# A recommender model on one core: the end of the GRU loop with its last softmax blocks in PSUM, an item term by TensorE and the last poolings divided differently

## The chip, the cores and the metric

The kernel runs on one core of one Trainium2 chip. The metric is the device time of one execution in microseconds, less being better. A core has TensorE (PE in the profile, its weight loads PEld), VectorE (DVE), ScalarE (ACT), GpSimd (POOL) and SyncE (SP), each with its own queue of instructions, which it works off in order; they meet through semaphores. Operands lie in SBUF, 128 partitions wide, or in PSUM, eight banks into which TensorE writes. In this kernel GpSimd works on SBUF alone.

## What is computed

1024 users have a history of 100 items, each a vector of 128. A GRU runs over the history, an attention gives each step a score against a target item, a masked softmax over the steps weights the GRU's states, and the pooled result sets the update gate of a second recurrence (AUGRU) over the same states. A small network makes the final score. Cut to what matters here:

```python
_, gru_seq = jax.lax.scan(gru_step, h0, jnp.swapaxes(item_historical_embedding, 0, 1))
keys = jnp.swapaxes(gru_seq, 0, 1)
q = jnp.broadcast_to(item_embedding[:, None, :], keys.shape)
feat = jnp.concatenate([keys, q, keys - q, q * keys], axis=-1)
score = _mlp(feat, [(att_W0, att_b0), (att_W1, att_b1), (att_W2, att_b2)], jax.nn.relu)
score = jnp.where(mask[:, :, None] == 1, score, -jnp.inf)
attn = jax.nn.softmax(score, axis=1)[..., 0]
pooled = jnp.einsum('bt,btd->bd', attn, keys)
att_seq = pooled.T[:T]
...
_, aug_seq = jax.lax.scan(augru_step, h0, (jnp.swapaxes(keys, 0, 1), att_seq))
```

The first attention layer has a part that depends on the step (keys, and keys times item) and a part that depends on the item alone.

## The kernel before, in words

Features lie on the partitions and users along the free axis, in two halves of 512 users. The kernel has two phases. `gru_phase` runs 100 GRU steps over both halves (`Half.gru`), and beside them the attention, the softmax, the pooling, and what the final network can have early. `augru_phase` runs the second recurrence, which needs the pooled weights of all users: it starts with a store of `pooled` to memory, gathers of its rows, and their spreading by TensorE. The schedule is written by hand: the order of the calls in the source is the order in each engine's queue.

The attention of a step takes three rounds. `attend(t)` lets TensorE make, in 32-column blocks that share one bank per half, the first layer of step t (`wk` with the state, `wkq` with the product state times item), the second layer of step t-1 and the third of step t-2, all in one pass over the `mv` of the round before. `take(t)` reads the result: up to step 99 VectorE adds the item part `q0`, which was made once for all steps with its bias (L684, `f`), ScalarE applies the Relu (L689, `mv`), and the finished score of step t-2 goes by DMA on SP from a row of `mv` into `s_b` (L696). The rounds T and T+1 finish the last two steps; there ScalarE reads the bank itself, with a bias (L691).

The softmax goes by blocks of steps whose ends are in `ENDS`: the last are 90 to 93, 93 to 96, 96 to 98 and 98 to 100. A block has three stages: scores of half 0, scores of half 1 with the maxima, and, after an exponential on ScalarE, the sums. As the maximum can rise, a block also gives a factor by which what has been pooled so far is scaled. `Half.pool` then works off a list per half: a scaling (L576) when a block begins, and for each step a product of the transposed state with the weight (L586) and an addition to `pooled` (L587), the two called a pair below. Each half has its own part of `pooled`, in which the additions follow one another. Within the loop GpSimd pools.

After the loop six PSUM banks are taken over, `b[0]` to `b[5]`. The blocks 96 to 98 and 98 to 100 then have their weights `e` in PSUM (`banks["e"]`; named `last` in the profile) and are copied to SBUF at the end of their sums (L773), so that VectorE pools from PSUM and GpSimd from SBUF. The block 93 to 96 is begun inside the loop and has its `e` in SBUF; a copy of it to PSUM is made for VectorE (L885). Half 0 is then pooled by GpSimd and half 1 by VectorE (L890 to L914). Between these, TensorE makes the features of the final network (L617, `some`), and the last transposes of the state are made (L537). At the end VectorE masks `pooled` into `s_b` (L919), and SP and ScalarE send the result to memory.

Whether VectorE or GpSimd works off an entry, and where, is said by calls such as these:

```python
halves[0].pool(T, nc.gpsimd)
halves[1].pool(1, nc.vector)
stage()
```

The count is the number of steps to pool at most; scalings on the way are not counted.

Of the kernel before, what the change touches and what calls it, by code (L numbers as in the profile page):

```python
# [9 lines left out]
F32 = mybir.dt.float32  # L10
# [9 lines left out]
P = 128  # L20
B = 1024
T = 100
HB = 512
# [6 lines left out]
NK = B // R  # L30
# [7 lines left out]
QA, QB = (2, 3), (3, 2)  # L38
# [10 lines left out]
ENDS = (*range(8, 81, 8), 86, 90, 93, 96, 98, T)  # L49


G = 4
# [20 lines left out]
def kernel(ctx: ExitStack, tc: tile.TileContext, a: dict, out: bass.AP):  # L73
# [26 lines left out]
    nc = tc.nc  # L100
# [22 lines left out]
    item = const.tile([P, B], F32, name="item")  # L123
# [47 lines left out]
    def gru_phase(pools):  # L171
# [18 lines left out]
        wk, wkq, wq, w12, bm = [], [], [], [], []  # L190
# [447 lines left out]

        banks = {}

        def attend(t):

            p = left[t] = [pa.tile([P, HB], F32, tag="a", name="pm") for _ in halves]

            old = [half.mv if t else hist[:, half.cols] for half in halves]
            k_rows = slice(0 if t <= T else 2 * R, P)

            def pack(i, q, w, v, start, stop):
                s = ts(q, R)
                nc.tensor.matmul(p[i][s, :], lhsT=w[:, s], rhs=v, start=start, stop=stop)  # L650

            def first(i, q, j):
                if t < T:
                    w = (wk, wkq)[j][i]
                    pack(i, q, w, halves[i].first[j], j == 0 and q != QB[i], j == 1)

            def more(i, q):
                pack(i, q, w12[i][k_rows, :], old[i][k_rows, :], True, q == QA[i] or t >= T)

            for turn in range(2 * NH):  # L660
                i, j = divmod(turn, 2)
                for q in range(2):
                    first(i, q, j)
                if i == 0:
                    for q in range(2, P // R):
                        more((QA, QB)[j].index(q), q)
                else:
                    for q in range(2, P // R):
                        first(QB.index(q), q, j)
# [1 line left out]
        blocks = [0, *ENDS]  # L671
        soft = {"stages": [], "exp": None, "j": 0}

        def take(t):

            if t < 0:
                return
            p = left.pop(t)
            rows = slice(0 if t < T else 2 * R, P)
            sums = []  # L680
            for half in halves:
                if t < T:
                    sums.append(wp.tile([P, HB], F32, name="f"))
                    nc.vector.tensor_add(sums[-1], p[half.i], q0[:, half.cols])  # L684
            for half in halves:
                half.mv = wp.tile([P, HB], F32, name="mv", bufs=4)
                to, of, bias = half.mv[rows, :], p[half.i][rows, :], bm[half.i][rows, :]
                if t < T:
                    nc.scalar.activation(to, sums[half.i], AF.Relu)  # L689
                else:  # L690
                    nc.scalar.activation(to, of, AF.Relu, bias=bias)  # L691
            s, j = t - 2, soft["j"]
            if s < 0:
                return
            for half in halves:
                nc.sync.dma_start(  # L696
                    out=s_bs[NH * (j % 2) + half.i].rearrange("(p r) f -> p r f", r=R)[
                        :, s - blocks[j], :
                    ],
                    in_=half.mv[SC[half.i] : SC[half.i] + 1, :]  # L700
                    .unsqueeze(1)
                    .to_broadcast([1, P // R, HB]),
                )
            if s == blocks[j + 1] - 1:
                softmax()


        def softmax():

            j = soft["j"]  # L710
            b0, b1 = blocks[j], blocks[j + 1]
            n, last = b1 - b0, b1 == T
            rows = n + (1 if j else 0)
            on = later["on"][:, :, b0:b1]
            top_old, den_old = soft.get("top"), soft.get("den")
            e = sp.tile([P, NK, 2 * G + 1], F32, name="e", bufs=3)
            both = e, None
            if banks:

                b = banks["e"].pop()  # L720
                both = e, b[:, : NK * (G + 1)].rearrange("p (k n) -> p k n", n=G + 1)
                e = both[1]
                top_n, den_n = (b[:, NK * m : NK * (m + 1)] for m in range(G + 1, G + 3))
            top = sp.tile([P, NK], F32, name="top", bufs=3)
            den = sp.tile([P, NK], F32, name="den", bufs=3)
            if both[1] is None:
                top_n, den_n = top, den
            soft.update(j=j + 1, top=top, den=den, e=both)

            def scores(i):  # L730
                ks = ts(i, KH)
                if banks:
                    pt = blocked(banks["pt"])
                else:
                    pt = pa.tile([P, KH, R], F32, tag="a", name="pt")
                nc.vector.transpose(
                    pt, s_bs[NH * (j % 2) + i].rearrange("p (k r) -> p k r", r=R)
                )

                nc.vector.tensor_mul(e[:, ks, :n], pt[:, :, :n], on[:, ks, :])  # L740

            def tops():
                scores(1)
                nc.vector.tensor_reduce(top_n, e[:, :, :n], AX.X, ALU.max)
                if j:
                    nc.vector.tensor_max(top, top_n, top_old)
                    nc.vector.tensor_sub(e[:, :, n], top_old, top_n)
                    if both[1] is not None:
                        nc.vector.tensor_scalar_min(e[:, :, n], e[:, :, n], 0.0)
                nc.vector.tensor_sub(  # L750
                    e[:, :, :n], e[:, :, :n], top.unsqueeze(2).to_broadcast([P, NK, n])
                )
                soft["exp"] = exponents

            def exponents():
                nc.scalar.activation(e[:, :, :rows], e[:, :, :rows], AF.Exp)

            def sums():
                nc.vector.tensor_mul(e[:, :, :n], e[:, :, :n], on)  # L759
                nc.vector.tensor_reduce(den_n, e[:, :, :n], AX.X, ALU.add)  # L760
                if j:
                    old = sp.tile([P, NK], F32, name="old")
                    nc.vector.tensor_mul(old, den_old, e[:, :, n])
                    nc.vector.tensor_add(den, den_n, old)
                if last:
                    nc.vector.reciprocal(den, den)
                    nc.vector.tensor_mul(
                        e[:, :, :rows],
                        e[:, :, :rows],
                        den.unsqueeze(2).to_broadcast([P, NK, rows]),  # L770
                    )
                if both[1] is not None:
                    nc.vector.tensor_copy(both[0][:, :, :rows], e[:, :, :rows])  # L773
                for half in halves:
                    if j:
                        half.todo.append((both, n, None))
                    half.todo += [(both, t - b0, t) for t in range(b0, b1)]

            soft["stages"] += [lambda: scores(0), tops, sums]

        def stage(count=1):
            for _ in range(count):
                if soft["stages"]:
                    soft["stages"].pop(0)()
# [72 lines left out]
        all_of(rest)  # L857

        b = [ps.tile([P, HB], F32, tag="g", name="last") for _ in range(6)]
        banks.update(e=[b[0], b[1]], kw=b[3], pt=b[2], f=[b[4], b[5]])  # L860

        features = [half.features(g) for half in halves for g in range(GH)]

        def some(*these):
            for f in these:
                next(features[f])

        take(T - 2)
        for half in halves:
            half.product(T - 1)  # L870
        attend(T - 1)
        stage(2)
        weights = soft["e"][0]
        exponents()
        some(0, 1)
        take(T - 1)
        some(0, 1)
        attend(T)
        some(2)
        for half in halves:  # L880
            half.transpose(T - 1)
        stage()
        n = ENDS[-3] - ENDS[-4] + 1
        copy = banks["e"][0][:, : NK * n].rearrange("p (k n) -> p k n", n=n)
        nc.vector.tensor_copy(copy, weights[:, :, :n])  # L885
        for half in halves:
            half.todo = [
                ((w[0], copy if w[0] is weights else None), n, t) for w, n, t in half.todo
            ]
        halves[0].pool(T, nc.gpsimd)  # L890
        halves[1].pool(1, nc.vector)
        stage()
        take(T)
        some(2)
        attend(T + 1)
        some(3, 4)
        stage()
        take(T + 1)
        exponents()
        some(3, 4)  # L900
# [8 lines left out]
        stage(2)  # L909
        exponents()  # L910
        some(7)
        stage()
        halves[0].pool(T, nc.gpsimd)
        halves[1].pool(T, nc.vector)  # L914


        for half in reversed(halves):
# [372 lines left out]
```

## Time and profile before

| what | us |
|---|---|
| median of 5 runs | 2089.94 |
| lowest and highest of them | 2086.67, 2091.57 |
| the profiled execution | 2088.85 |
| its span in the profile | 2087.1 |
| last GRU state written (L527) | 1413.08 |
| VectorE's last work of the first phase (L919) begins | 1446.70 |
| VectorE's first work of the second phase (L973) | 1461.40 |

A line of the timeline has the start in us from the span's beginning, the duration in us, the engine, the line of the kernel, the operation, output and inputs with their shapes, and a count. Brackets give how long the engine was idle before and what released it. Equal neighbours are merged, so that an x2 stands for two instructions. An instruction can begin while the end of the one before it is still counted, so what lies from one start to the next is used for chains of them. In a row of a stretch, the busy time of each engine is followed by its count of instructions.

### The profile page before, as it was taken

How to read it: one execution, taken by the hardware profiler on the slowest of the kernel's cores; microseconds unless marked ns; L12 is line 12 of the kernel's file. 1: busy time of each engine (PE TensorE's matmuls, PEld its weight loads, DVE VectorE, ACT ScalarE, POOL GpSimd, SP SyncE). 2: the span in 40 equal slices, each digit the busy share in tenths (PEclk: the TensorE clock that was granted, in tenths of full speed). 3: DMA queues.
4: the chain of work that ended last, by engine and by line, in shares of the span. 5: the costliest groups of instructions: out<-in, count | busy, mean ns of one | idle time of the engine just before them, and what ended most of it. 6: DMA issues, size and time to landing. Idle time of an engine off the chain costs nothing. (4 is left out here: it accounts for less than half of the span.)

```text
span 2087.1 us, 26811 instructions
## 1 busy us (share of the span) xinstructions
PE 2040.4 (98%) x8320; PEld 981.4 (47%) x8320; DVE 1753.7 (84%) x3050; ACT 832.3 (40%) x1516; POOL 1308.9 (63%) x1306
## 2 busy tenths in 40 slices
PE   8999999999999999999999999997899999999997
PEld 3343333333333333333333333333444556679887
DVE  6888999999989888989888899997467777888786
ACT  3334343433434333433343343343344444455454
POOL 0334939579796959595969687986635444444232
PEclk9999999999999999999999999999999999999999
DMA  4643233332234334333433232332534333334231
GB/s 118 114 93 99 91 103 110 95 103 84 87 103 111 114 98 121 110 100 104 133 108 91 82 92 79 101 93 74 148 95 111 97 93 96 98 98 100 74 73 35
DMA packets 254324, 205.09 MB, mean 98 GB/s; under 512 B 75814, under 2 KB 216842, under 8 KB 254170
## 3 DMA queue, kind: packets, MB, share of 16 engines
q1 hardware_dynamic: 239738, 170.57, 29.4%
q0 software_dynamic: 12320, 32.44, 5.6%
q8 instruction: 68, 1.11, 0.2%
q14 instruction: 86, 0.70, 0.1%
q10 hardware_dynamic: 2112, 0.26, 0.1%
HBM read 147.16 MB, written 54.40 MB: 97 GB/s over the span
## 5 line engine op out<-in xcount | busy, mean ns | idle before, releaser
L490 PE MATMUL ps<-x,wih 128*128 128x512 f32 x1200 | 592.6, 603 | 4.2 <-DMA x<-in_hist_x 4.2
L490 PE MATMUL ps<-hn,whh 128*128 128x512 f32 x1188 | 574.4, 592 | 0.0
L490 PEld LDWEIGHTS ps<-x,wih 128*128 128x128 f32 x1200 | 220.9, 191 | 327.7 <-issue 253.2
L490 PEld LDWEIGHTS ps<-hn,whh 128*128 128x128 f32 x1188 | 225.7, 190 | 284.1 <-issue 275.3
L476 POOL TENSOR_TENSOR xm<-x,m 128x512 f32<-128x512 f32 x200 | 248.6, 1243 | 135.2 <-DMA m<-mask_d 134.9
L521 ACT ACTIVATE ps<-ps,bih 128x512 f32<-128x512 f32 x200 | 132.4, 662 | 480.2 <-DVE ps L520 480.2
L502 ACT ACTIVATE r<-ps,brz 128x512 f32<-128x512 f32 x200 | 137.5, 687 | 380.8 <-PE ps L490 380.2
L477 POOL TENSOR_TENSOR hist<-hist,xm 128x512 f32<-128x512 f32 x200 | 269.0, 1345 | 15.7
L586 POOL TENSOR_TENSOR kw<-kt,e 128x512 f32<-128x512 f32 x191 | 219.5, 1149 | 70.3 <-DVE e L759 70.2
L587 POOL TENSOR_TENSOR pooled<-pooled,kw 128x512 f32<-128x512 f32 x191 | 254.0, 1330 | 15.0
L159 POOL DMA_INDIRECT rows<-keys_d,idx_k x208 | 202.8, 975 | 83.8 <-POOL rows L158 51.5
L563 DVE TENSOR_TENSOR kq<-hn,item 128x512 f32<-128x512 f32 x200 | 226.5, 1171 | 0.0
L650 PE MATMUL pm<-hn,wk 128*32 128x512 f32 x1200 | 211.6, 596 | 3.5 <-ACT q L233 1.8
L650 PE MATMUL pm<-kq,wkq 128*32 128x512 f32 x1200 | 209.2, 592 | 0.0
L1032 ACT ACTIVATE c<-ph,bh 128x96 f32<-128x96 f32 (+42 forms) x198 | 96.9, 489 | 263.3 <-PE ph L1024 229.7
L650 PE MATMUL pm<-mv,w 128*32 128x512 f32 (+1 forms) x808 | 195.8, 598 | 0.6 <-DVE e L740 0.6
L158 POOL COPY rows<-rest 128x1 f32<-128x1 f32 x208 | 39.4, 190 | 224.1 <-DVE rest L1061 219.9
L1048 DVE TENSOR_TENSOR pu<-pu,c 128x96 f32<-128x96 f32 (+42 forms) x197 | 88.8, 451 | 105.1 <-ACT c L1032 89.5
L684 DVE TENSOR_TENSOR f<-pm,q 128x512 f32<-128x512 f32 x200 | 128.3, 683 | 51.8 <-PE pm L650 51.8
L525 DVE TENSOR_TENSOR d<-hn,ps 128x512 f32<-128x512 f32 x198 | 136.0, 687 | 34.8 <-ACT ps L521 32.5
L526 DVE TENSOR_TENSOR d<-ps,d 128x512 f32<-128x512 f32 x200 | 138.3, 691 | 23.7 <-ACT ps L522 6.8
L520 DVE TENSOR_TENSOR ps<-ps,u 128x512 f32<-128x512 f32 x200 | 140.0, 700 | 21.6 <-PE ps L490 0.5
(180 smaller groups left out, 3031.4 us busy)
## 6 DMA issues: line engine op xcount, KB each, us to landing
x<-in_hist_x SPq DMA_DIRECT2D x212, 256.0 KB
keys_d<-kt SPq DMA_DIRECT2D x46, 1024.0 KB
m<-mask_d SPq DMA_DIRECT2D x200, 128.0 KB
keys_d<-kt SPq DMA_DIRECT2D x64, 64.0 KB
rows<-keys_d,idx_k POOLq DMA_INDIRECT x208
s_b<-mv SPq DMA_DIRECT2D x200, 8.0 KB
mask_i<-in_mask SPq DMA_DIRECT2D x8, 200.0 KB
at<-att_d SPq DMA_DIRECT2D x32, 48.0 KB
```

What stands on the lines that cost most here:

```text
L159: nc.gpsimd.indirect_dma_start(out=r[:, k, :], out_offset=None, in_=keys_d[q], in_offset=bass.IndirectOffsetOnAxis(ap=idx_k[:, k, i : i + ...
L476: nc.gpsimd.tensor_mul(d, x, m)
L477: nc.gpsimd.tensor_add(acc, acc, d)
L490: nc.tensor.matmul(p, lhsT=w[:, g, :], rhs=v, start=(j == 0), stop=(j == len(parts) - 1),)
L502: nc.scalar.activation(r, pr, AF.Sigmoid, bias=brz[:, 0:1])
L520: nc.vector.tensor_add(pi, pi, u)
L525: nc.vector.tensor_sub(d, h, pi)
L526: nc.vector.tensor_mul(d, pz, d)
L563: nc.vector.tensor_mul(kq, h, item[:, self.cols])
L586: eng.tensor_mul(d, k, w)
L587: eng.tensor_add(acc, acc, d)
L650: nc.tensor.matmul(p[i][s, :], lhsT=w[:, s], rhs=v, start=start, stop=stop)
```

## The change

- The block 93 to 96 no longer begins inside the loop (the test behind L704 leaves its end out); `softmax()` is called for it after the loop, when the banks are there. So its scores, maxima, weights and sums lie in PSUM, and the copy at the end of its sums goes to SBUF. L885 and what belongs to it goes.
- Three blocks need three places for `e`: one bank is divided in two for the blocks 93 to 96 and 96 to 98. The last block uses `b[0]`.
- The attention of the last step, `attend(T - 1)`, gets banks of its own (`b[0]` and `b[3]`) instead of the two used in turn. TensorE adds the item part to them first, six 32-column matmuls of `wq` with `item`; `take(T - 1, own=True)` therefore has no addition by VectorE, and ScalarE reads the banks with the bias.
- This `take` now stands ahead of the exponential of the block 93 to 96 in ScalarE's queue, where it stood behind it. `attend(T)` moves ahead of the second `some(0, 1)`, which holds copies by ScalarE alone, so TensorE's own order stays.
- Of the block 93 to 96, step 94 of half 1 is pooled by GpSimd, behind its three steps of half 0. VectorE keeps the steps 93 and 95.
- Of the last block, VectorE pools the last step of half 0, which was GpSimd's. VectorE pools the block 96 to 98 of half 1 ahead of the last block's sums instead of behind them.

```diff
@@ attend @@
-        def attend(t):
+        def attend(t, own=None):
-            p = left[t] = [pa.tile([P, HB], F32, tag="a", name="pm") for _ in halves]
+            p = left[t] = own or [pa.tile([P, HB], F32, tag="a", name="pm") for _ in halves]
...
                     w = (wk, wkq)[j][i]
-                    pack(i, q, w, halves[i].first[j], j == 0 and q != QB[i], j == 1)
+                    start = j == 0 and q != QB[i] and own is None
+                    pack(i, q, w, halves[i].first[j], start, j == 1)
             def more(i, q):
-                pack(i, q, w12[i][k_rows, :], old[i][k_rows, :], True, q == QA[i] or t >= T)
+                start = own is None or q == QA[i]
+                pack(i, q, w12[i][k_rows, :], old[i][k_rows, :], start, q == QA[i] or t >= T)
+            if own is not None:
+                for i, q in ((0, 0), (0, 1), (0, QB[0]), (1, QB[1]), (1, 0), (1, 1)):
+                    pack(i, q, wq[i], item[:, halves[i].cols], True, False)
@@ take @@
-        def take(t):
+        def take(t, own=False):
...
-                if t < T:
+                if t < T and not own:
                     sums.append(wp.tile([P, HB], F32, name="f"))
                     nc.vector.tensor_add(sums[-1], p[half.i], q0[:, half.cols])
...
-                if t < T:
+                if sums:
                     nc.scalar.activation(to, sums[half.i], AF.Relu)
                 else:
                     nc.scalar.activation(to, of, AF.Relu, bias=bias)
...
-            if s == blocks[j + 1] - 1:
+            if s == blocks[j + 1] - 1 and s != ENDS[-3] - 1:
                 softmax()
@@ softmax @@
-                both = e, b[:, : NK * (G + 1)].rearrange("p (k n) -> p k n", n=G + 1)
+                both = e, b[:, : NK * G].rearrange("p (k n) -> p k n", n=G)
                 e = both[1]
-                top_n, den_n = (b[:, NK * m : NK * (m + 1)] for m in range(G + 1, G + 3))
+                top_n, den_n = (b[:, NK * m : NK * (m + 1)] for m in range(G, G + 2))
@@ gru_phase, after the loop @@
-        banks.update(e=[b[0], b[1]], kw=b[3], pt=b[2], f=[b[4], b[5]])
+        two = [b[1][:, ts(j, HB // 2)] for j in range(2)]
+        banks.update(e=[b[0], *two], kw=b[3], pt=b[2], f=[b[4], b[5]])
...
+        softmax()
         take(T - 2)
         for half in halves:
             half.product(T - 1)
-        attend(T - 1)
+        attend(T - 1, [b[0], b[3]])
         stage(2)
-        weights = soft["e"][0]
+        take(T - 1, own=True)
         exponents()
         some(0, 1)
-        take(T - 1)
+        attend(T)
         some(0, 1)
-        attend(T)
         some(2)
         for half in halves:
             half.transpose(T - 1)
         stage()
-        n = ENDS[-3] - ENDS[-4] + 1
-        copy = banks["e"][0][:, : NK * n].rearrange("p (k n) -> p k n", n=n)
-        nc.vector.tensor_copy(copy, weights[:, :, :n])
-        for half in halves:
-            half.todo = [
-                ((w[0], copy if w[0] is weights else None), n, t) for w, n, t in half.todo
-            ]
         halves[0].pool(T, nc.gpsimd)
         halves[1].pool(1, nc.vector)
-        stage()
+        halves[1].pool(1, nc.gpsimd)
         take(T)
         some(2)
         attend(T + 1)
         some(3, 4)
-        stage()
+        stage(2)
         take(T + 1)
         exponents()
...
         stage(2)
         exponents()
         some(7)
+        halves[1].pool(T, nc.vector)
         stage()
-        halves[0].pool(T, nc.gpsimd)
+        halves[0].pool(1, nc.gpsimd)
         halves[1].pool(T, nc.vector)
+        halves[0].pool(T, nc.vector)
```

## The prediction

> **What bounds the kernel now.** I read the page first, then the stretches around the change, then each engine's timeline there. The page's chain of waits covers only the output's last microseconds and says nothing of this place.
>
> ```profile
> PE 2040.4 (98%) x8320; PEld 981.4 (47%) x8320; DVE 1753.7 (84%) x3050; ACT 832.3 (40%) x1516; POOL 1308.9 (63%) x1306
> ```
>
> Over the span TensorE leads. The change sits between the GRU loop's last step and the second recurrence, and there the order is another:
>
> ```profile
> 1413.00:1423.00 10.00, 8.58 (x51) 4.04 (x53) 9.68 (x19) 4.12 (x8) 4.00 (x4) 1.00 0.01 3
> 1423.00:1434.00 11.00, 10.51 (x54) 7.17 (x51) 10.42 (x22) 4.15 (x10) 6.95 (x6) 1.00 0.16 48
> 1434.00:1448.00 14.00, 4.19 (x21) 3.17 (x20) 12.90 (x32) 1.98 (x5) 11.34 (x10) 0.72 0.58 175
> ```
>
> Busy columns: PE, PEld, DVE, ACT, POOL. VectorE is busy 33.0 of these 35 us. Its timeline from 1413.1 to 1447.99 has one idle entry, 0.30 us. So this stretch is as long as VectorE's instructions in their order, and a wait put into that order lengthens it.
>
> ```profile
> 1422.35 0.65 DVE L759 TENSOR_TENSOR e<-e,on 128x96 f32<-128x96 f32 x1
> 1423.20 1.02 DVE L763 TENSOR_TENSOR old<-den,e 128x32 f32<-128x32 f32 x1
> 1424.25 1.29 DVE L764 TENSOR_TENSOR den<-den,old 128x32 f32<-128x32 f32 x1
> 1434.04 0.19 DVE L763 TENSOR_TENSOR old<-den,last 128x32 f32<-128x32 f32 x1
> 1437.87 0.23 DVE L759 TENSOR_TENSOR last<-last,on 128x64 f32<-128x64 f32 x1 [0.30 <-ACT last L756]
> 1446.70 1.29 DVE L919 TENSOR_TENSOR s_b<-used,pooled 128x512 f32<-128x512 uint8 x2
> ```
>
> The same line costs 1.02 us with both operands in SBUF and 0.19 us with one in PSUM ("last"). GpSimd and ScalarE beside it:
>
> ```profile
> 1421.80 1.08 POOL L576 TENSOR_TENSOR pooled<-pooled,e 128x512 f32<-128x512 f32 x1 [5.80 <-ACT e L756]
> 1428.99 1.27 POOL L587 TENSOR_TENSOR pooled<-pooled,kw 128x512 f32<-128x512 f32 x1
> 1434.76 1.08 POOL L576 TENSOR_TENSOR pooled<-pooled,e 128x512 f32<-128x512 f32 x1 [4.50 <-DVE e L773]
> 1420.09 1.28 ACT L756 ACT_TABLE_LOAD   x1 [4.46 <-DVE e L750]
> 1418.34 1.04 PE L650 MATMUL pm<-kq,wkq 128*32 128x512 f32 x8
> ```
>
> GpSimd has 4.5 us of room after its three pairs (1430.26 to 1434.76), none later. Behind the stretch everything hangs on VectorE's end:
>
> ```profile
> 1446.72 2.07 PE L947 MATMUL pu<-k,wu 128*128 128x512 f32 x2 [6.96 <-DVE pooled L587]
> 1461.40 0.70 DVE L973 TENSOR_TENSOR first<-first,first_u 128x512 f32<-128x512 f32 x1 [13.40 <-PE first L962]
> ```
>
> SP's pooled stores start at 1447.42 (the first L919 just done), ScalarE's at 1448.03, the gathers at 1453.30, and VectorE's next work at 1461.40. TensorE's L947 too waits for VectorE's last L587. So I carry a shift of VectorE's end one to one.
>
> **The change, part by part.** Times are on the profile's clock, and lines are those of before. The changed program's order of instructions shows no difference ahead of 1412 us.
>
> *Item part by TensorE.* Removed: two L684 sums, 1.20 us on VectorE (1419.93 to 1421.13). Added: six 32-column matmuls. A quarter of an attention (four such at once) has a pitch of 0.86 us (1417.48 to 1418.34), and six need two of these, 1.72 us. Cover: before, TensorE stands idle 1.71 us ahead of this attention (its work ends at 1412.71, the next begins at 1414.42) because it waits for L684 to free a bank. The new banks are free at 1409.3 and 1410.0, so the six fit, price nothing; without that cover, 1.72. The attention still ends at 1419.38, because its second quarter waits for kq and the mv of ScalarE. ScalarE then reads PSUM itself: start 0.10 later (0.09 and 0.12 at two L691 pairs), two Relus 1.25, to 1420.73. Queued behind them now are the table load, 1.30 with its gap, and the exponential, 0.30: done at 1422.33, where it was 1421.72. VectorE, which has 3.03 of scores and tops (block 96 to 98 takes 2.95 with a column less) and 1.22 of transposes after 1417.07, is ready at 1421.32 and waits 1.05. The 1.20 saved is therefore given back almost whole: L759 starts at 1422.37, against 1422.35. Bounds: 1421.75 if the load could lie where it does now (-0.6), 1424.1 with the six exposed (+1.7). I take 1422.37, since the new order has the Relus first.
>
> *Block 93 to 96 in PSUM.* L759 to the copy took 3.50 (1422.35 to 1425.85). The same instructions of the next block, in PSUM with a copy to SBUF, take 1.02 (1433.51 to 1434.53); with one more column 1.08. So VectorE comes to L576 at 1423.45 instead of 1425.85: a gain of 2.40. The copy made by L885 goes and one for GpSimd comes, both inside these sums, and the extra minimum (L749, 0.23) is inside the 3.03.
>
> The reduction's rows speak for an equal fixed price: L744 from SBUF 0.25 with 96 elements, L760 from PSUM 0.23 with 64. [...]
>
> *GpSimd's start.* It used to begin on e at 1421.80, straight after the exponential. Now it waits for VectorE's copy; in the next block it starts 0.39 after that copy begins. So 1423.70, 1.90 later.
>
> *The pooling shared anew.* VectorE's L576 and first pair on half 1 take 1.93, to 1425.38. The scores of block 96 to 98 follow (2.95, to 1428.33). Their mv DMAs leave when the Relus end at 1420.73, 4.65 earlier; 5.03 was enough before, and SP's last store, issued until 1449.4, had released ScalarE by 1450.34. Then comes the pair for step 95 of half 1: its product at about 1429.1 (the new order makes it wait for the second block's exponential, behind Relus ending at 1428.82), its sum at 1429.85 at the earliest. But step 94 of half 1 is now GpSimd's, and adds to the same sums, so this addition must wait for it, and the order of the changed program indeed shows a wait on GpSimd there. GpSimd does it after half 0: 1.04 for L576 and four pairs at 2.38 (1423.07 to 1425.45) make 10.56, so it ends at 1434.30. VectorE adds at 1434.40, after 4.55 us idle, and is through at 1435.01, where before the stretch of pairs ended at 1433.51: +1.50. Queued behind are all of block 96 to 98's sums, GpSimd's next e, and the last block. The bound below is 1063 + 1262 ns a pair, the shortest rows (-0.2); above, 1539 + 1612 ns, the longest (+3.2). I take the pitch of the nearest rows.
>
> From there before needed 14.48 (to 1447.99). After: sums 1.02, last scores 2.95 (the 0.39 spent until the exponential goes, two pairs being put there), L576 and pairs 3.48 and 3.50, sums and copy 1.85, one more pair for half 0 1.44, L919 1.29: 15.53. End at **1450.54, 2.55 us later**. The last addition waits for GpSimd again; by the same steps GpSimd ends at 1447.9 and VectorE comes at 1448.5, so it costs nothing, with 0.6 to spare.
>
> Sum: -2.40 up to the end of the scores of block 96 to 98 (1428.33 against 1430.73); +3.90 over the pairs behind them (0.77 for the exponential, 0.75, 4.55 idle and 0.61 make 6.68, against 2.78 for two pairs before); +1.05 from there; together +2.55. SP's order of transfers is unchanged. The profiled execution took 2088.85 (span 2087.10 and 1.75 around it) and would take 2091.4. It lies 1.09 under the median of the five runs, so for a median I add to 2089.94: **2092.4**.
>
> The two weight blocks share one bank. [...]
>
> **Rivals.**
> - *Slower: GpSimd's chain runs long.* Place: the four pairs before the shared addition. For it: such pairs reached 1.53 and 1.60 around 1403 while VectorE ran kq, and every microsecond goes straight to the end. Against: in this stretch VectorE's remaining instructions have at most one SBUF operand, and beside such the pairs kept 2.38. At the longest rows, 4 x 0.8 = 3.2: 2095.6. It decides from a GpSimd end of 1436.0, 1.7 later than mine. The six matmuls exposed would give 2094.1.
> - *Faster: the shared addition doesn't wait.* VectorE would go on at 1429.85, 4.55 sooner: 2.0 below before, 2087.9. For it: 4.5 us of GpSimd room seem to be there. Against: that room is taken up by the later start (1.90) and the pair (2.38), and GpSimd would have to end by 1429.8.
> - *Nothing arrives.* The gathers and ScalarE's load could have slack of their own: 2089.9. Against: the idle entries above end on VectorE's work or on transfers that begin with it.
>
> **How the numbers follow.** Forecast 0.66, its own range 2090.5 to 2094.5 (the bounds -0.8 and +1.7, and a median's wandering, the five runs spanning 4.9); long chain 0.20; no wait 0.08; nothing arrives 0.06. The range for eight in ten takes the long chain's centre in and leaves most of the no-wait case out: 2088.5 to 2096.0. The line of 0.2%, about what a measurement of this kernel can tell from no change, is 4.2 us: 2085.8 and 2094.1. Slower: most of the long chain and a tenth of mine, 0.27. Faster: 0.05, since even the no-wait case stops short of it. The rest, 0.68, is within.
>
> **What would show it.** VectorE idle about 4.5 us before an L587, released by POOL pooled; about 1 us idle before the block's mask product, released by ScalarE; GpSimd's first L576 near 1423.7 and no pause before its second; L763 at 0.19 throughout; the two L919 ending near 1450.5. Wrong if the shared addition finds GpSimd done, if GpSimd's pairs leave 2.38, or if the second recurrence starts at 1461.4 regardless.

## The result, and the profile after

The changed kernel took 2092.80 us (median of 23 runs, 2088.09 to 2097.38), the kernel before 2088.82 us (median of 43 runs on the same chip). The ratio is 1.0018, with an interval of 1.0013 to 1.0024, which is 3.8 us more (2.7 to 5.0); the two medians alone differ by 3.98. The profiled execution took 2094.48 us, with a span of 2092.7.

Behind the edited lines the changed kernel's numbers are shifted: L684, L691, L756, L759, L763 and L773 of before are L690, L697, L762, L765, L769 and L779, and L919 and L973 are L921 and L975. L586 and L587 stay. In the variants below they move by a few lines more; the operands tell them apart.

The page's first part, for the changed kernel:

```profile
PE 2044.6 (98%) x8332; PEld 984.1 (47%) x8332; DVE 1752.8 (84%) x3049; ACT 831.4 (40%) x1516; POOL 1304.2 (62%) x1306
```

TensorE has the twelve matmuls more (each of the six is issued as two), VectorE one instruction less. Over the whole span nothing else is to be seen. By stretches (busy time of PE, PEld, DVE, ACT and POOL, each with its count; then granted clock and DMA):

```profile
1413.00:1423.00 10.00, 10.00 (x67) 4.19 (x60) 9.21 (x18) 3.78 (x6) 4.01 (x4) 1.00 0.02 4
1423.00:1434.00 11.00, 11.00 (x59) 7.59 (x58) 6.41 (x18) 5.04 (x13) 8.90 (x8) 1.00 0.22 67
1434.00:1448.00 14.00, 3.20 (x18) 2.54 (x16) 11.72 (x31) 1.98 (x5) 9.40 (x10) 0.67 0.52 159
```

These rows stand at the same times as those of before, though in this execution the last L527 comes 1.16 us later (1414.24 against 1413.08). In the middle row VectorE falls from 10.51 us of before to 6.41. It has less to do there, and it stands. Where, the waits of the changed kernel between 1414 and 1452 us tell (all of VectorE's; total, number, longest):

```profile
DVE pooled L587 <- POOL pooled L587: 4.4, 1, 4.4
DVE last L765 <- ACT last L762: 1.0, 1, 1.0
DVE last L586 <- ACT last L762: 0.7, 1, 0.7
```

The same engine's timeline shows what stands around them:

```profile
1414.24 0.69 DVE L527 TENSOR_TENSOR hn<-ps,d 128x512 f32<-128x512 f32 x1
...
1423.57 0.27 DVE L765 TENSOR_TENSOR last<-last,on 128x96 f32<-128x96 f32 x1 [0.98 <-ACT last L762]
...
1424.17 0.19 DVE L769 TENSOR_TENSOR old<-den,last 128x32 f32<-128x32 f32 x1
1424.39 0.19 DVE L770 TENSOR_TENSOR den<-last,old 128x32 f32<-128x32 f32 x1
1424.50 0.28 DVE L779 COPY e<-last 128x128 f32<-128x128 f32 x1
...
1430.36 0.70 DVE L586 TENSOR_TENSOR last<-kt,last 128x512 f32<-128x512 f32 x1 [0.70 <-ACT last L762]
1435.48 0.69 DVE L587 TENSOR_TENSOR pooled<-pooled,last 128x512 f32<-128x512 f32 x1 [4.43 <-POOL pooled L587]
...
1449.63 0.69 DVE L587 TENSOR_TENSOR pooled<-pooled,last 128x512 f32<-128x512 f32 x1
1450.23 1.28 DVE L921 TENSOR_TENSOR s_b<-used,pooled 128x512 f32<-128x512 uint8 x2
...
1464.92 0.70 DVE L975 TENSOR_TENSOR first<-first,first_u 128x512 f32<-128x512 f32 x1 [13.40 <-PE first L964]
```

The two sums on `old` and `den` now cost 0.19 us each, where they cost 1.02 and 1.29. Against that stand the three waits, 6.11 us. From the start of L527 to the end of L921 it is 37.27 us (1451.51 less 1414.24), against 34.91 before (1447.99 less 1413.08): **2.36 us more**. I call this the stretch. From its end to L975 it is 13.41 us in both kernels.

GpSimd's timeline shows the engine that VectorE waits for:

```profile
1424.86 1.08 POOL L576 TENSOR_TENSOR pooled<-pooled,e 128x512 f32<-128x512 f32 x1 [7.69 <-DVE e L779]
1425.89 1.07 POOL L586 TENSOR_TENSOR kw<-kt,e 128x512 f32<-128x512 f32 x1
...
1434.18 1.27 POOL L587 TENSOR_TENSOR pooled<-pooled,kw 128x512 f32<-128x512 f32 x1
1437.28 1.07 POOL L576 TENSOR_TENSOR pooled<-pooled,e 128x512 f32<-128x512 f32 x1 [1.82 <-DVE e L779]
...
1447.75 1.26 POOL L587 TENSOR_TENSOR pooled<-pooled,kw 128x512 f32<-128x512 f32 x1
```

It begins when VectorE's copy to `e` is there, 10.62 us after L527 begins, and needs one scaling (1.03) and four pairs with a pitch (from the start of one to the start of the next) of 2.38. The fourth pair ends at 1435.45, and VectorE adds at 1435.48. GpSimd's last addition ends at 1449.01, 0.62 us before VectorE's own last one begins (1449.63). ScalarE, which sets the first wait:

```profile
1420.70 1.26 ACT L697 ACTIVATE mv<-last,bm 128x512 f32<-128x512 f32 x2 [3.91 <-PE last L651]
1421.98 1.28 ACT L762 ACT_TABLE_LOAD   x1
1423.27 0.26 ACT L762 ACTIVATE last<-last 128x128 f32<-128x128 f32 x1
```

The Relus, the table load and the exponential follow without a gap, so the load is whole on the path. TensorE, with the new item part:

```profile
1413.67 1.89 PE L651 MATMUL last<-item,wq 128*32 128x512 f32 x12
...
1419.51 1.04 PE L651 MATMUL last<-kq,wkq 128*32 128x512 f32 x8
```

The twelve lie in the gap that TensorE had, and the attention ends 6.31 us after L527 begins (1420.55), where it was 6.30.

### The profile page after: what moved, and what is told of

It reads as the page before. It is cut to its first block, busy times and chain, and to the rows that moved or that the text cites. A ratio compares the mean times of both kernels' runs of the same rounds, so it can differ in the third digit from the quotient of the medians.

```text
span 2092.7 us, 26832 instructions
## 1 busy us (share of the span) xinstructions
PE 2044.6 (98%) x8332; PEld 984.1 (47%) x8332; DVE 1752.8 (84%) x3049; ACT 831.4 (40%) x1516; POOL 1304.2 (62%) x1306
## 5 line engine op out<-in xcount | busy, mean ns | idle before, releaser
L477 POOL TENSOR_TENSOR hist<-hist,xm 128x512 f32<-128x512 f32 x200 | 266.5, 1333 | 15.7
L587 POOL TENSOR_TENSOR pooled<-pooled,kw 128x512 f32<-128x512 f32 x191 | 254.4, 1332 | 15.0
L586 POOL TENSOR_TENSOR kw<-kt,e 128x512 f32<-128x512 f32 x191 | 219.6, 1150 | 70.1 <-DVE e L765 70.0
L690 DVE TENSOR_TENSOR f<-pm,q 128x512 f32<-128x512 f32 x198 | 127.0, 683 | 50.7 <-PE pm L651 50.4
L520 DVE TENSOR_TENSOR ps<-ps,u 128x512 f32<-128x512 f32 x200 | 140.0, 700 | 21.6 <-PE ps L490 0.5
```

What stands on the lines that cost most here:

```text
L477: nc.gpsimd.tensor_add(acc, acc, d)
L520: nc.vector.tensor_add(pi, pi, u)
L586: eng.tensor_mul(d, k, w)
L587: eng.tensor_add(acc, acc, d)
```

## The experiments

All were profiled. "Shared addition" is VectorE's first L587 behind GpSimd's step of half 1; it and GpSimd's start on the block 93 to 96 are counted from the start of the last L527. The difference is the ratio to the kernel before, run beside it on the same chip, times that kernel's median. "Not shared", "half 1 first" and "item by VectorE" ran on one chip, with the changed kernel repeated beside them (median 2086.58 us); "table early", "block in SBUF" and "all mended" ran on a second, without it; "last pair by GpSimd" and "before, delayed" ran on a third, each with the changed kernel beside it (2093.05 and 2092.73).

| kernel | stretch | GpSimd's start | shared addition | ratio (interval) | difference, us |
|---|---|---|---|---|---|
| before | 34.91 | 8.72 | none | | |
| changed | 37.27 | 10.62 | 21.24 | 1.0018 (1.0013 to 1.0024) | 3.8 (2.7 to 5.0) |
| not shared | 34.33 | 10.61 | none | 0.9997 (0.9988 to 1.0006) | -0.6 (-2.5 to 1.3) |
| half 1 first | 33.43 | 10.62 | 16.92 | 0.9998 (0.9989 to 1.0007) | -0.4 (-2.3 to 1.5) |
| item by VectorE | 37.33 | 10.72 | 21.36 | 1.0013 (1.0004 to 1.0022) | 2.7 (0.8 to 4.6) |
| table early | 36.18 | 9.53 | 20.15 | 1.0003 (0.9994 to 1.0012) | 0.6 (-1.2 to 2.5) |
| block in SBUF | 36.08 | 9.42 | 20.11 | 1.0003 (0.9994 to 1.0012) | 0.6 (-1.2 to 2.5) |
| last pair by GpSimd | 38.35 | 10.63 | 21.28 | 1.0033 (1.0021 to 1.0045) | 6.9 (4.4 to 9.4) |
| before, delayed | 39.56 | 8.71 | none | 1.0024 (1.0015 to 1.0033) | 5.0 (3.1 to 6.9) |
| all mended | 32.30 | 9.52 | 15.10 | 0.9987 (0.9978 to 0.9996) | -2.7 (-4.5 to -0.8) |

In the changed kernel, in "item by VectorE", "table early" and "block in SBUF", which differ in what sets GpSimd's start, the stretch is that start and 26.61 to 26.66 us more. That one number carries most of what follows.

**Not shared.** VectorE pools all three steps of half 1 again; the rest is as changed.

```diff
         halves[1].pool(1, nc.vector)
-        halves[1].pool(1, nc.gpsimd)
         take(T)
```

> The changed kernel, but step 94 of half 1 stays with VectorE, so nothing of the block 93 to 96 is shared. Measure: the stretch, from the start of the last L527 to the end of the last L921 (34.91 us before, 37.27 changed). If the wait of the shared addition is the cost: VectorE's idle 4.43 us goes, a pair of 1.44 comes back, the stretch falls by 2.96 to about 34.3, and the time by 3.0 us against the changed kernel (about 0.6 under before, if the rest of the difference lies in this stretch). If the cost lies in the blocks in PSUM, the six matmuls or the extra pair at the end: the stretch stays near 37.3 and the time with it.

Measured: 34.33. VectorE's waits between 1414 and 1452 us in this kernel are the other two alone:

```profile
DVE last L765 <- ACT last L762: 1.0, 1, 1.0
DVE last L586 <- ACT last L762: 0.7, 1, 0.7
```

So the sharing costs 2.94 us (37.27 less 34.33), more than the whole difference to before, and the other parts together gain 0.58. The median (2082.88) is 3.70 under that of the changed kernel on the same chip.

**Half 1 first.** The sharing stays, but GpSimd does its step of half 1 ahead of half 0.

```diff
         stage()
-        halves[0].pool(T, nc.gpsimd)
         halves[1].pool(1, nc.vector)
         halves[1].pool(1, nc.gpsimd)
+        halves[0].pool(T, nc.gpsimd)
```

> The changed kernel with the same work on the same engines; only GpSimd's order differs: step 94 of half 1 ahead of half 0's three steps. Wait theory: GpSimd's addition for half 1 ends near 1428.1 on the changed profile's clock, before VectorE needs it at 1431.1, so the 4.43 us idle goes and only the 0.70 for the exponential stays. Half 0 ends 2.4 later on GpSimd, which the last addition feels by about 0.2. Stretch 33.1 (37.27 - 4.40 + 0.25), time 4.1 us under the changed kernel and 1.8 under before if nothing else differs. If the division of work itself costs (too much for VectorE or for GpSimd), the order changes nothing: 37.3.

Measured: 33.43. VectorE's timeline in this kernel:

```profile
1432.17 0.69 DVE L586 TENSOR_TENSOR last<-kt,last 128x512 f32<-128x512 f32 x1 [0.70 <-ACT last L762]
1432.96 0.69 DVE L587 TENSOR_TENSOR pooled<-pooled,last 128x512 f32<-128x512 f32 x1
...
1447.58 0.69 DVE L587 TENSOR_TENSOR pooled<-pooled,last 128x512 f32<-128x512 f32 x1 [0.57 <-POOL pooled L587]
```

The wait of 4.43 us is gone, and 0.57 has come at the last addition, where I had about 0.25. GpSimd's timeline shows where the rest comes from:

```profile
1428.65 1.28 POOL L587 TENSOR_TENSOR pooled<-pooled,kw 128x512 f32<-128x512 f32 x1 [0.92 <-DVE pooled L587]
```

Its addition of the shared step now waits 0.92 us for VectorE's first one, so half 0 begins 3.22 us later than in the changed kernel (13.84 after L527's start) and not the 2.4 that I had. It was thus the place of the shared step in GpSimd's queue, not the sharing itself: so placed, sharing beats not sharing by 0.90 us. The two medians (2083.51 and 2082.88) can't tell that apart; the stretch can. Both lie under the changed kernel's median on this chip (2086.58), by 3.07 and 3.70 us.

**Item by VectorE.** The item part goes back to two additions by VectorE, and the attention of the last step to the old banks and the old place of its `take`.

```diff
-        attend(T - 1, [b[0], b[3]])
+        attend(T - 1)
         stage(2)
-        take(T - 1, own=True)
         exponents()
         some(0, 1)
+        take(T - 1)
```

> The changed kernel with the item part of the last step back on VectorE (two sums L690) and the exponential back ahead of the Relus. My step: the six matmuls gained nothing, since the 1.20 us they took from VectorE came back as a wait for ScalarE (0.98 idle). So VectorE's first masked product begins 0.15 later, stretch 37.4, time equal within 0.2 us. Rival: the sums' 1.20 us were saved in full, then this is 1.2 slower (38.5); or the matmuls and the longer ScalarE queue cost, then it is faster.

Measured: 37.33. The wait of 0.98 before L765 goes, the additions come back, and GpSimd starts 0.10 later. That part of the change, additions and order put back together, is worth 0.06 us where GpSimd's start sets the end.

**Table early.** A small exponential on a spare column stands behind the Relus of the step before, so that ScalarE's table load lies there.

```diff
         take(T - 2)
+        nc.scalar.activation(table, table, AF.Exp)
```

> The changed kernel with one more ScalarE instruction, an exponential on one column right after the Relus of step 98, so that the table load lies in ScalarE's idle time before the last step's Relus. If the 0.98 us that VectorE waits before the block 93 to 96's masked product is that load, the wait is gone, and since GpSimd's start and so the shared addition hang on it, the whole stretch falls by 1.0: 36.3 us against 37.27, and the time by 1.0. The 0.70 wait for the second exponential grows to about 1.7 and lies ahead of the shared addition's wait, which stays near 4.4 less what it grew. If the start of that product is set by something else (the Relus themselves, TensorE), nothing changes: 37.3.

Measured: 36.18. The block's exponential now follows the last step's Relus without a load (1423.70, the Relus beginning at 1422.55); in "all mended", which has the same line, the load stands behind the Relus of the step before, at 1416.06 with 1.28 us. VectorE's waits in its timeline:

```profile
1432.21 0.69 DVE L586 TENSOR_TENSOR last<-kt,last 128x512 f32<-128x512 f32 x1 [1.79 <-ACT last L762]
1436.24 0.69 DVE L587 TENSOR_TENSOR pooled<-pooled,last 128x512 f32<-128x512 f32 x1 [3.34 <-POOL pooled L587]
```

VectorE no longer waits at L765 and comes 1.09 us sooner to the next product, which has to wait 1.09 longer (1.79). At the shared addition the gain stays, because GpSimd started 1.09 sooner and its four pairs set the end. A gain in a wait counted here only as far as it moved GpSimd's start.

**Block in SBUF.** The block 93 to 96 begins inside the loop again and has its weights in SBUF, with the copy to PSUM for VectorE; item part and sharing are as changed.

```diff
-            if s == blocks[j + 1] - 1 and s != ENDS[-3] - 1:
+            if s == blocks[j + 1] - 1:
                 softmax()
...
-        banks.update(e=[b[0], *two], kw=b[3], pt=b[2], f=[b[4], b[5]])
+        banks.update(e=[b[0], b[1]], kw=b[3], pt=b[2], f=[b[4], b[5]])
...
-        softmax()
         take(T - 2)
...
+        nc.vector.tensor_copy(copy, weights[:, :, :n])
```

> The changed kernel with only the block 93 to 96 put back in SBUF, as it was before, with its copy to PSUM for VectorE; item part, shared step and last pair as changed. By itself that undoes a gain of 2.40 us on VectorE. Wait theory: VectorE comes later by about 2.4 to its poolings, but GpSimd again begins right at the exponential, 0.9 to 1.2 us sooner, and it is GpSimd's end that releases VectorE: the idle shrinks to about 2 us and the stretch FALLS, by 0.9, to 36.3. Rival: VectorE's instructions set the stretch here too, then it is 2.4 longer: 39.7.

Measured: 36.08. GpSimd's timeline in this kernel, and then VectorE's:

```profile
1423.29 1.15 POOL L576 TENSOR_TENSOR pooled<-pooled,e 128x512 f32<-128x512 f32 x1 [6.49 <-ACT e L762]
1424.40 1.07 POOL L586 TENSOR_TENSOR kw<-kt,e 128x512 f32<-128x512 f32 x1
```

```profile
1423.24 0.26 DVE L765 TENSOR_TENSOR e<-e,on 128x96 f32<-128x96 f32 x1 [1.21 <-ACT e L762]
...
1423.71 0.80 DVE L769 TENSOR_TENSOR old<-den,e 128x32 f32<-128x32 f32 x1
1424.54 0.97 DVE L770 TENSOR_TENSOR den<-den,old 128x32 f32<-128x32 f32 x1
...
1430.57 0.23 DVE L756 TENSOR_TENSOR last<-last,top 128x64 f32<-128x64 f32 x1
1430.71 0.69 DVE L586 TENSOR_TENSOR last<-kt,last 128x512 f32<-128x512 f32 x1
1433.98 0.69 DVE L587 TENSOR_TENSOR pooled<-pooled,last 128x512 f32<-128x512 f32 x1 [2.59 <-POOL pooled L587]
```

VectorE's sums are dear again (0.80 and 0.97 instead of 0.19 each), and still the end is 1.19 us sooner. For GpSimd starts straight on the exponential's result, 1.20 sooner than where it must wait for VectorE's copy, and VectorE had its dear sums while it would have stood. The saving of 2.40 us which the prediction found in the block was real, but lay on an engine that went on to wait.

The product L586 at 1430.71 follows its predecessor without a wait. In the changed kernel it waited 0.70 us for the exponential of the other block, whose weights it doesn't read but which lies in the same bank. Here that block has a bank of its own, and its exponential begins only at 1430.83, while the product runs.

**Last pair by GpSimd.** The last step of half 0 goes back to GpSimd.

```diff
-        halves[0].pool(1, nc.gpsimd)
+        halves[0].pool(T, nc.gpsimd)
         halves[1].pool(T, nc.vector)
-        halves[0].pool(T, nc.vector)
```

> The changed kernel with the last step of half 0 back on GpSimd, so that VectorE has one pair less at the end (1.44 us). If VectorE's count of work were what matters, the stretch falls by 1.44 to 35.8. By my steps GpSimd's two pairs then end 5.86 after its last scaling starts, at 1451.4 on the changed profile's clock, and VectorE's mask product for half 0 waits for that: stretch 37.9, 0.6 longer, time 0.6 above the changed kernel.

Measured: 38.35, 0.45 above the 37.9 expected. GpSimd's timeline at the end, and then VectorE's:

```profile
1446.43 1.07 POOL L586 TENSOR_TENSOR kw<-kt,e 128x512 f32<-128x512 f32 x1
...
1448.81 1.52 POOL L586 TENSOR_TENSOR kw<-kt,e 128x512 f32<-128x512 f32 x1
```

```profile
1448.66 0.73 DVE L920 TENSOR_TENSOR s_b<-used,pooled 128x512 f32<-128x512 uint8 x1
1451.70 0.69 DVE L920 TENSOR_TENSOR s_b<-used,pooled 128x512 f32<-128x512 uint8 x1 [2.31 <-POOL pooled L587]
```

The 0.45 is the second product, 1.52 us instead of 1.07, beside VectorE's mask product. So this division, which the change made anew, gains 1.08 us in the stretch (38.35 less 37.27). The difference in time, 6.9 us, is more than the stretch explains (3.44), and its interval leaves that out. Beside the changed kernel it was 3.26 us slower by the medians, where the stretch gives 1.08; the rest I can't place.

**Does the stretch carry one to one?** The kernel before, with eight additions by VectorE on two spare banks ahead of L919, which change nothing in what is computed:

```diff
         halves[1].pool(T, nc.vector)
+        for n in range(8):
+            nc.vector.tensor_add(b[2 + n % 2], b[2 + n % 2], q0[:, :HB])
```

> The kernel before, with eight extra additions of 512 columns on VectorE ahead of its mask products, whose results nobody uses; a pure delay of the stretch, by the pitches in this trace (0.61 to 0.72 us each) 4.9 to 5.8 us, so a stretch of 39.8 to 40.7. Theory: the second phase follows the stretch one to one, so the time is 4.9 to 5.8 above before. Rival: a longer stretch costs more than itself, as 3.8 and 3.6 us for 2.36 suggest (a factor of 1.5 to 1.6); then it is 7.4 to 9 above before.

Measured: 39.56, 4.65 above before and a little under the 39.8 expected, as the eight have a pitch of 0.60. VectorE's timeline:

```profile
1447.17 4.88 DVE L916 TENSOR_TENSOR last<-last,q 128x512 f32<-128x512 f32 x8
...
1466.64 0.70 DVE L974 TENSOR_TENSOR first<-first,first_u 128x512 f32<-128x512 f32 x1 [13.40 <-PE first L963]
```

The distance to the next phase's first work is 13.40 again, and the time rose by 5.0 us (3.1 to 6.9). One to one lies inside; a factor of 1.5 or more (7.0 us) lies outside.

**All mended.** Half 1 first, the table early, the block 96 to 98 in a bank of its own, and its exponential ahead of the last Relus.

```diff
-        banks.update(e=[b[0], *two], kw=b[3], pt=b[2], f=[b[4], b[5]])
+        banks.update(e=[two[0], b[0], two[1]], kw=b[3], pt=b[2], f=[b[4], b[5]])
...
         take(T - 2)
+        nc.scalar.activation(table, table, AF.Exp)
...
-        halves[0].pool(T, nc.gpsimd)
         halves[1].pool(1, nc.vector)
         halves[1].pool(1, nc.gpsimd)
+        halves[0].pool(T, nc.gpsimd)
...
         stage(2)
-        take(T + 1)
         exponents()
+        take(T + 1)
```

> The changed kernel with all its waits taken on: GpSimd does half 1's step first; the table is loaded early; the second block's exponential stands ahead of the last Relus; the second block's weights have a bank of their own, and the third shares with the first. Wait theory: VectorE has no wait until the last addition; there GpSimd, now busy without a pause, is 1.4 us late. Stretch 32.4 us (33.43 of the kernel with half 1 first, less 1.0), time 2.5 us under before and 4.9 under the changed kernel, so the fastest of all. If the division of work were at fault, it would stay above before (34.9).

Measured: 32.30, and 0.9987 of the kernel before. VectorE's waits in this kernel:

```profile
1430.80 0.73 DVE L742 STREAM_TRANSPOSE last<-s_b 128x512 f32<-128x512 f32 x1 [0.49 <-DMA s_b<-mv]
...
1443.91 0.69 DVE L587 TENSOR_TENSOR pooled<-pooled,last 128x512 f32<-128x512 f32 x1 [0.76 <-POOL pooled L587]
```

The three waits of the changed kernel are gone. I had not foreseen the first of the two left: VectorE now comes before the DMA of the last scores has landed. Compared with "half 1 first", its copy ahead of this line begins 1.83 us sooner after L527's start (16.56 against 18.39), and the last Relus, behind the exponential, begin 0.18 later (14.75 against 14.57). This is the one version that beats the kernel before, by 0.13%. It was not run beside the changed kernel; its stretch is 4.97 us shorter than that one's.

**Repeats.** The changed kernel was run again beside the experiments, on two chips, and the kernel before once more, on another chip, for its profile.

> The changed kernel unaltered, beside the others on one chip. The stretch accounts for +2.36 us of the difference of the two profiles (5.6); the loop ahead of it gave 1.16 and the second phase 2.08, of which 0.95 in its first step, where TensorE's matmuls took twice their time for 0.9 us longer. If these are a run's chance, this profile's loop and second phase agree with before within a microsecond or so and the time is 2.4 above before; if the second phase is truly later by the change, it shows the same 2 us again and the time is 4 above.

> The changed kernel once more beside before, for the size alone: 3.8 us (2.7 to 5.0) in the first comparison and 2.5 (0.6 to 4.4) in the second, where the stretch gives 2.36. If all of it is the stretch, about 2.4 again; if the second phase adds something of its own, 3.5 or more.

> The changed kernel beside the delayed one on one chip: stretch 37.3. One to one: 2.4 above before and 2.5 to 3.4 under the delayed kernel. With the factor: 3.6 above before and 4 to 5 under the delayed kernel.

> The kernel before unaltered, for a second profile of its loop and second phase. Stretch 34.9 as in the first. If the loop's and the second phase's parts of the difference between the first two profiles (1.16 and 2.08 us) were chance, these parts differ here by as much from the first profile.

Measured: stretches of 37.27, 37.29 and 37.28 for the changed kernel and 34.90 for before, where the first profiles had 37.27 and 34.91. The ratios to before were 1.0012 (1.0003 to 1.0021), 1.0016 (1.0008 to 1.0025) and 1.0014 (1.0005 to 1.0023), that is 2.5, 3.3 and 2.9 us more. Against the delayed kernel the last of them was 1.68 us faster by the medians, where 2.5 to 3.4 was expected and the stretches differ by 2.28.

## Why the prediction was right

| step | predicted | measured |
|---|---|---|
| end of the attention, after L527's start | 6.30 | 6.31 |
| wait at the mask product for ScalarE | 1.05 | 0.98 |
| GpSimd's start, after L527's start | 10.62 | 10.62 |
| wait for the second exponential | 0.77 | 0.70 |
| GpSimd's pitch | 2.38 | 2.38 |
| wait at the shared addition | 4.55 | 4.43 |
| spare at the last addition | 0.6 | 0.62 |
| stretch against before | +2.55 | +2.36 |
| median against before | +2.5 | +3.8 (2.7 to 5.0) |

*Item part by TensorE.* Price nothing and gain given back: shown. The attention ends where it did (6.31 against 6.30), and with VectorE's additions put back the stretch moved by 0.06 us only. The 1.20 us went into the wait for ScalarE, whose order the prediction had read off: Relus, load, exponential.

*Block in PSUM.* The block became cheaper as predicted. What I didn't draw from it is that the 2.40 us could not reach the end, since at the shared addition VectorE waits anyway, and that GpSimd's later start, which the prediction put at 1.90 us, was the price. Of these 1.90, the experiment with the block back in SBUF gives 1.20 to the block; the other 0.70 (9.42 there, 8.72 before) goes with the rest of the change, in which the exponential stands behind the Relus. By the same experiment, this part by itself lengthened the stretch by 1.19, as long as the shared step is last in GpSimd's queue. In the prediction's sum both effects are in, as the -2.40 and within the +3.90.

*The price of a PSUM source.* The prediction read an equal price from the reduction's rows, 0.25 us from SBUF and 0.23 from PSUM, though with 96 elements and 64. With 96 on both sides the rows lie 0.01 to 0.02 us apart: the mask product (L765) took 0.27 us from PSUM in the changed kernel and 0.26 from SBUF with the block put back, and the reduction behind it (L766) 0.27 against 0.25.

*The wait on the shared bank.* The prediction has the product at 1429.1 wait for the other block's exponential, with 0.77 us in the sum; no row of before shows that wait. The changed kernel's row shows it, with 0.70, and it goes when the block has its own bank: the product follows its predecessor without a wait at 1430.71 with the block in SBUF, and at 1427.81 in "all mended". The two blocks are halves of one tile, though, so the runs don't tell a wait for the bank from one for the tile. The wait cost nothing here, under the longer wait of 4.43; where that one is gone, as in "half 1 first", VectorE still stands these 0.70 us.

*Pooling shared anew.* The decisive step, and shown from two sides: taken away it gives 2.94 us back, put at the head of GpSimd's queue 3.84 (37.27 less 33.43). The medians on that chip fall with it, by 3.70 and 3.07.

*One sign was wrong.* I wrote that GpSimd would not pause before its second L576. It paused 1.82 us for VectorE's copy. My own sum had this pause, from the shared addition at 1434.40 to the sums and the copy behind it; the list of signs did not follow it.

*The size.* In the stretch the terms were 0.19 us too long: 0.08 up to the shared addition, 0.11 behind it. For the time I had 2.5 and measured 3.8, 2.5, 3.3 and 2.9. That the forecast of 2092.4 lies only 0.4 from the measured 2092.80 is partly luck: it set out from a median of five runs, 2089.94, where 43 runs gave 2088.82, and the difference came out larger by about as much. (Its last sum is also off by 0.1: 2089.94 and 2.55 are 2092.49.) The first interval, 2.7 to 5.0, leaves the stretch's 2.36 just out, the other three hold it. The first pair of profiles differed by 5.6 us, of which the stretch is 2.36, the loop ahead of it 1.16 and the second phase 2.08. But the loop is the same code in both, and took 1413.08 and 1414.73 in two profiles of before, and 1414.24, 1412.75, 1413.48 and 1413.59 in four of the changed kernel. So that part of the first pair's difference is one execution's chance; whether something small besides the stretch remains, half a microsecond or one, these runs don't tell.

*The rivals.* The long chain did not come: four pairs in this stretch kept 2.38. It was near, though: the product at 1.52 in the last-pair experiment is just such a lengthening. The case that the addition finds GpSimd done did not come either, and became true when GpSimd's order was turned. That nothing arrives is refuted by the 13.40 before L975 in every kernel in which it was moved, except 13.57 and 13.69 in two.

## What to carry to other kernels

When two engines add to one sum in turn, put the shared step at the head of the helping engine's queue: at its end it cost 2.94 us here, at its head it gained 0.90, even though the helping engine then waited 0.92 for the first engine's addition. A saving counts only up to the next wait on another engine, so ask first which start sets the end; here four kernels ended 26.61 to 26.66 us after GpSimd's start, whatever VectorE had saved. And undo each part of a change alone: one that looked like its best, the block in PSUM, lengthened the stretch by 1.19 in the order in which it stood.

## What the hardware showed besides

*VectorE with two operands in SBUF, beside GpSimd.* With the block in SBUF, VectorE's L769 ended at 1424.51, just as GpSimd's L576 did (1424.44), and its L770 at 1425.51, just as GpSimd's product did (1425.47). Both work on 32 elements and take 0.19 us where one operand is in PSUM. In the last-pair experiment it went the other way: VectorE's mask product ran until 1449.39, and GpSimd's product, begun at 1448.81, took 1.52 us instead of 1.07. The kernel before has one instruction in both cases, 96 elements with both operands in SBUF:

```profile
1381.56 1.35 DVE L750 TENSOR_TENSOR e<-e,top 128x96 f32<-128x96 f32 x1
...
1419.76 0.26 DVE L750 TENSOR_TENSOR e<-e,top 128x96 f32<-128x96 f32 x1
```

At the first, GpSimd's L477 ran from 1381.45 to 1382.79, and VectorE's instruction ended at 1382.91; at the second GpSimd was idle (1416.00 to 1421.80). With one operand in PSUM, L763 and L764 of the same kernel took 0.19 us each at 1438.41 and 1438.63, while GpSimd's product ran (1438.17 to 1439.25). So in these rows the price of those sums is mostly a wait for the other engine's instruction rather than work, and what PSUM saved was that wait.

*Chips differ.* The kernel before took 2083.54 us on one chip, 2066.68 on another, and 2088.82 to 2090.06 in the other comparisons, yet on the second the stretch was 34.90, as in the first profile (34.91). Nor was the loop shorter there (1414.73 to the last L527, against 1413.08). The difference is in the second phase. ScalarE's timeline has this line in the first profile of before:

```profile
1476.22 0.59 ACT L1007 COPY k<-pk 128x512 f32<-128x512 f32 x1 [8.02 <-PE pk L1006]
```

and the same instruction in the profile of before on the second chip:

```profile
1468.47 0.58 ACT L1007 COPY k<-pk 128x512 f32<-128x512 f32 x1 [1.27 <-PE pk L1006]
```

This copy of `k` (the one ahead of it is at 1455.29 and 1456.93) begins 14.82 us after L973 in the one (1461.40) and 5.43 in the other (1463.04). That is 9.4 of the 21.6 us between the two spans (2087.1 and 2065.5); most of the rest lies later in the second phase. The distance goes with the chip and not with the kernel: it is 5.43 us in all four profiles from the second chip, "all mended" among them, and 14.22 to 14.88 in the ten others. What makes it was not tried. It is a reason to compare times only between runs on one chip.
